# Folding the bias of v through one channel, and moving two small steps of the first batch

## The chip, the cores and the metric

The kernel runs on one core of a Trainium2 chip. A core has a matrix engine (TensorE, PE in the profile), a vector engine (VectorE, DVE), a scalar engine (ScalarE, ACT), a general engine (GpSimd, POOL) and a queue engine (SyncE, SP) that here only issues DMAs. Each engine runs its own instructions strictly in order and waits on semaphores for the others. The metric is the device time of one execution in microseconds (us), the median of several runs.

## The reference

The input x has 8 batches of 1024 rows and 256 channels. All in float32:

```
xn  = layernorm(x)                       # over the 256 channels, no scale or shift
qkv = xn @ qkv_w + qkv_b                 # 16 heads of 16 channels each
q, k = q/|q|, k/|k|                      # per row and head
kv  = einsum('bhnd,bhne->bhde', k, v)    # linear attention, no softmax
att = einsum('bhnd,bhde->bhne', q, kv) @ proj_w + proj_b
ffn = relu(xn @ W1 + b1) @ W2 + b2       # 256 -> 1024 -> 256
out = x + att + ffn
```

Since there is no softmax, v is never formed. With kn the normalised k, the kernel computes G = xn^T kn (256 x 256), then kv = Wv^T G + b_v (sum of kn). The bias term is had by changing both factors. If xn gets 1 added in some channels and the rows of Wv get a row vector a added, the product gains what b_v needs. It rests on the channels of xn summing to zero in every row, so that adding the same a to every row of Wv changes nothing by itself.

## The kernel before, in words

Rows are tiled by 128: a batch is 8 tiles, two halves of four. The large products (the hidden layer, the output, q and k, G) are made by a Strassen-like scheme with seven products in place of eight, called here "by sums": POOL builds sums and differences of blocks ahead of the matmuls, DVE adds the products together as they leave PSUM. Names in the trace: `pq*` are banks of the q/k projection, `ph*` of the hidden layer, `po*` of the output, `gp*` of G.

The program is one list written out by hand; the order in which the Python code issues instructions is the order on every engine. There is no planner.

Batch 0 is special. A prologue warms PE, normalises x of batch 0 on DVE and projects q and k in plain matmuls (`project`, L326). DVE adds the bias (L333), ACT squares (L342), DVE reduces the squares to sums per head (L343), and DVE also takes the statistics of the first half of batch 1 (L255, L258) meanwhile. Then comes `hidden(0)`, which walks a list of steps: `first(i)`, `fifth(i)` and `last(i)` for the four units i of the hidden layer (matmuls L658, DVE adds L670, ACT copies L684 and ReLUs L665). Behind each step the dictionary `first_steps` names small work to be issued: the norms of k (`norms_of_first`: L368 maximum on DVE, L371 square root on ACT, L374 reciprocal on DVE), the scaling of k and q by them on POOL (`scale`, L489), the normalisation of batch 1 (`norm_scale`: L267 and L270 on DVE; `norm_apply`: L279 on ACT), the addition of ones to x (`shift`, L518 on ACT), G of batch 0 in plain matmuls (`mix_g`, L525), the fold of v's bias (`fold_bias_of_v`: L505 on PE, L508 and L512 on DVE), the transposes of batch 1 (`turn_x`: L293 on DVE, L295 DMAs from SP), kv (`mix_kv`: L619 on PE, L625 on DVE) and M = kv proj_w (`mix_m`: L636, L640). The sums for the hidden layer's output are POOL's (`sums_of_a`, L192 to L196), and so are those of W2 (L188), of wq and wk (L381, L188) and of x of batch 1 (L229 to L241).

`mix_g` of batch 0 is a join: its first matmul needs k scaled by POOL and x of batch 0 with the ones that `shift` adds on ACT. Its matmuls stand on PE behind the fifth product of unit 1.

Later batches use `later_steps` and `shift(b + 2)` at their end; they differ from batch 0 in order only.

Of the kernel before, what the change touches and what calls it, by code (L numbers as in the profile page):

```python
# [9 lines left out]
F32 = mybir.dt.float32  # L10
AF = mybir.ActivationFunctionType
ALU = mybir.AluOpType
# [4 lines left out]
def kernel(  # L17
# [34 lines left out]
    nc = tc.nc  # L52
    P = 128
    B, N, C = x.shape
    H, D = 16, 16
    assert H * D == C
    INTER = w1.shape[1]
    NT = N // P
    HT = NT // 2
# [30 lines left out]
    def bank(shape, name):  # L90

        return psum.tile(shape, F32, tag="bank", name=name)
# [15 lines left out]
    def load_squares(b, halves=(0, 1)):  # L108
        xqs[b] = one.tile([P, 2, R, HT, CJ], F32, tag="xq", name=f"xq_{b}")
        for n in halves:  # L110
            for j in range(R):
                nc.sync.dma_start(out=xqs[b][ts(j, S), n], in_=squares_v(x, b, n, j))
# [25 lines left out]
    w2_sb = const.tile([P, FC, C], F32, tag="w2", name="w2_sb")  # L138
    ob = const.tile([P, 3, 2], F32, tag="ob", name="ob")

    def load_halves(dst, w):

        src = w.rearrange("(k p) (j m c) -> m j p k c", p=P, m=2, c=S)
        for m in range(2):
            for j in range(R):
                nc.sync.dma_start(out=dst[:, :, (m * R + j) * S : (m * R + j + 1) * S], in_=src[m, j])

    def load_rest():

        load_halves(w2_sb, w2)  # L150
        load_halves(projw_sb, proj_w)
        for i, v in enumerate((proj_b, b2)):
            for j in range(R):
                nc.sync.dma_start(
                    out=ob[ts(j, S), i, :],
                    in_=v.rearrange("(j m c) -> j c m", m=2, c=S)[j],
                )
# [107 lines left out]
    def norm_scale(b, tiles, on_act):  # L265
        i, mv, rstd = stats[b, tiles[0]]
        nc.vector.reciprocal(rstd, rstd)  # L267
        if on_act:
            nmr = small.tile([P, NT], F32, tag="nmr", name=f"nmr_{b}_{i}")[:, : len(tiles)]
            nc.vector.scalar_tensor_tensor(nmr, mv[:, :, 0], -1.0, rstd, ALU.mult, ALU.mult)  # L270
            for t in tiles:
                stats[b, t] += (nmr,)

    def norm_apply(b, tiles):
        for t in tiles:
            xt, xn = xs[b][:, t, :], xns[b][:, t, :]
            i, mv, rstd, *nmr = stats.pop((b, t))
            if nmr:
                nc.scalar.activation(  # L279
                    xn, xt, AF.Identity, bias=nmr[0][:, i : i + 1], scale=rstd[:, i : i + 1]  # L280
                )
            else:
                nc.vector.tensor_scalar(
                    xn, xt, mv[:, i, 0:1], rstd[:, i : i + 1], ALU.subtract, ALU.mult
                )
# [23 lines left out]
    def project(b, within={}, behind={}, held_to=0):  # L309

        xnT = xnTs[b]
        if b not in qks:
            qks[b] = one.tile([P, NT, 2 * C], F32, tag="qk", name=f"qk_{b}")
        qk = qks[b]
        late, held, adds = [], [], []
        for h in range(2):
            ss = small.tile([P, HT, 2 * H], F32, tag="ssk" if h else "ssq", name=f"ss_{b}_{h}", bufs=1)
            for s in range(2):  # L320
                norms_of[b, h, s] = ss[:, :, ts(s, H)]
            for i in range(HT):
                t = h * HT + i
                pq = bank([P, 512], f"pq_{b}_{t}")
                for kc in range(KC):
                    nc.tensor.matmul(  # L326
                        pq, xnT[:, kc, t // 2, :, t % 2], wqkv_sb[:, kc, 0 : 2 * C],
                        start=(kc == 0), stop=(kc == KC - 1), skip_group_check=True,
                    )
                    if kc == 0:  # L330
                        within.get(t, lambda: None)()
                adds.append(
                    lambda t=t, pq=pq: nc.vector.tensor_tensor(  # L333
                        qk[:, t, :], pq, qkvb_sb[:, 0 : 2 * C], ALU.add
                    )
                )
                while adds and t > 0:
                    adds.pop(0)()

                def square(t=t, ss=ss, i=i):  # L340
                    sq = work.tile([P, 2 * C], F32, tag="yt", name=f"sq_{b}_{t}")
                    nc.scalar.activation(sq, qk[:, t, :], AF.Square)  # L342
                    return lambda: nc.vector.tensor_reduce(  # L343
                        ss[:, i, :], sq.rearrange("p (g d) -> p g d", d=D), AX.X, ALU.add
                    )

                held.append(square)
                while held and t >= held_to:
                    late.append(held.pop(0)())
                    while len(late) > 1:  # L350
                        late.pop(0)()
                behind.get(t, lambda: None)()
        while late:
            late.pop(0)()

    norms_of = {}

    def invert(ss):

# [3 lines left out]

    def norms_of_first(s):

        parts = [norms_of[0, h, s] for h in range(2)]
        for p in parts:
            nc.vector.tensor_scalar_max(p, p, L2_EPS * L2_EPS)  # L368
        yield
        for p in parts:  # L370
            nc.scalar.activation(p, p, AF.Sqrt)  # L371
        yield
        for p in parts:
            nc.vector.reciprocal(p, p)  # L374
        yield

# [109 lines left out]
    def scale(eng, b, h, s):  # L486

        part = qks[b][:, ts(h, HT), ts(s, C)].rearrange("p t (g d) -> p t g d", d=D)
        eng.tensor_tensor(  # L489
            part, part,  # L490
            norms_of[b, h, s].unsqueeze(3).to_broadcast([P, HT, H, D]), ALU.mult,
        )
# [8 lines left out]
    def fold_bias_of_v():  # L501

        wv = wqkv_sb[:, :, of_v]
        of_rows = bank([P, C], "of_rows")
        nc.tensor.matmul(of_rows, mean, wv[:, 0, :], start=True, stop=True)  # L505
        yield
        a = one.tile([P, C], F32, tag="ksum", name="a")
        nc.vector.scalar_tensor_tensor(  # L508
            a, qkvb_sb[:, of_v], 1.0 / P, of_rows, ALU.mult, ALU.subtract
        )  # L510
        yield
        nc.vector.tensor_tensor(wv, wv, a.unsqueeze(1).to_broadcast([P, KC, C]), ALU.add)  # L512
        yield

    def shift(b):

        part = xns[b][:, :, 0:P]
        nc.scalar.activation(part, part, AF.Identity, bias=ones)  # L518

    def mix_g(b):  # L520
        qk, xn = qks[b], xns[b]
        gp = ps_mix.tile([P, KC, C], F32, tag="mix", name=f"gp_{b}")
        for f in range(KC):
            for t in range(NT):
                nc.tensor.matmul(  # L525
                    gp[:, f, :], xn[:, t, ts(f, P)], qk[:, t, C : 2 * C],
                    start=(t == 0), stop=(t == NT - 1),
                )
        gT = one.tile([P, KC, C], F32, tag="gT", name=f"gT_{b}")
        nc.scalar.copy(gT, gp)  # L530
        mixes[b] = gT
# [206 lines left out]
    def first_steps(b):  # L738

        lo, hi, fold = range(HT), range(HT, NT), fold_bias_of_v()  # L740
        of_k, of_q = norms_of_first(1), norms_of_first(0)
        return {
            0: [lambda: load_squares(b), lambda: norm_apply(b + 1, lo)],
            1: [lambda: next(of_k)] * 3 + [lambda h=h: scale(nc.gpsimd, b, h, 1) for h in range(2)],
            2: [lambda: shift(b)],
            4: [
                lambda: norm_stats(b + 1, hi), lambda: norm_scale(b + 1, hi, True),
                lambda: norm_apply(b + 1, hi), lambda: next(of_q), lambda: next(of_q),
                lambda: next(of_q), lambda: mix_g(b), lambda: next(fold),
            ] + [lambda: turn_x(b + 1)] * R,  # L750
            5: [lambda: next(fold), lambda: next(fold), sums_of_wqk, sum_of_biases]
            + [lambda h=h: scale(nc.gpsimd, b, h, 0) for h in range(2)],
            6: [lambda: shift(b + 1)],
            7: [lambda: mix_kv(b)],
            8: [lambda: g_sums(b + 1, 0)],
            10: [lambda: mix_m(b), lambda: turn_q(b)],
            11: [lambda: turn_q(b), lambda: load(b + 2)],
        }
# [212 lines left out]
    def tiles_4_to_7():  # L971
# [8 lines left out]
    of_next = norm_stats_steps(1, range(HT))  # L980
    project(
        0, {0: tile_1, 1: tiles_2_3, 3: tiles_4_to_7},
        {t: lambda n=n: [next(of_next) for _ in range(n)] for t, n in ((3, 1), (4, 1), (5, 1), (6, 2))}
        | {7: lambda: norm_scale(1, range(HT), True)},
        3,
    )
    load_rest()
    s3_of_x(0)
    sums_of_w2()
# [71 lines left out]
```

## Time and profile before

| | before |
|---|---|
| median of 3 runs (lowest to highest) | 613.55 us (613.02 to 614.63) |
| profiled execution, its time | 613.64 us |
| its span, first to last instruction | 611.8 us |
| busy: PE | 605.9 us (99%) |
| busy: DVE | 419.4 us (69%) |
| busy: ACT | 208.2 us (34%) |
| busy: POOL | 422.0 us (69%) |
| granted PE clock, mean | 0.999 |

The span is what the profiler sees between the first and the last instruction; the time is some 1.8 us longer. A row of a timeline gives the start in us, how long the merged instructions took, engine, line, operation, what is written and read by the program's names, and the count; idle time of the engine ahead of it, and what ended that, stand in square brackets. A busy PE is one that has a matmul in flight: in PE's rows the start of the next pass says more than the end of this one.

### The profile page before, as it was taken

To read this page: it belongs to the slowest core of one execution; us is meant where nothing else is said; L and a number is where in the kernel's file an instruction comes from. 1 tells how busy PE (TensorE), PEld (TensorE's weight loads), DVE (VectorE), ACT (ScalarE), POOL (GpSimd) and SP (SyncE) were. 2 spreads that over 40 slices of the span, in tenths; PEclk is the share of its full clock that TensorE was granted. 3 is DMA by queue.
4 is the path that set the end of the run, shared out by engine and by line. 5 is a ranking of instruction groups with operands and counts; after the bars stand their busy time and mean duration, and the time that the engine had idled before them with its cause. 6 is when DMAs were issued, how large, how long until landed. Compare 5 with 4: busy or idle time off the path is not lost.

```text
span 611.8 us, 6697 instructions
## 1 busy us (share of the span) xinstructions
PE 605.9 (99%) x2037; PEld 349.6 (57%) x2037; DVE 419.4 (69%) x751; ACT 208.2 (34%) x362; POOL 422.0 (69%) x346
## 2 busy tenths in 40 slices
PE   9999999999999999999999999999999999999996
PEld 6466664465644756448464484644755556645454
DVE  7987767877487764787557784687846777258824
ACT  4645214441334413343143520526205352023500
POOL 2899992699636995479934999259991599914700
PEclk9999999999999999999999999999999999999999
DMA  8543403750048300581005810158002640005202
GB/s 286 84 101 74 104 1 69 167 108 0 1 99 188 58 1 5 126 175 40 0 19 120 181 27 0 34 127 167 19 0 48 140 90 0 1 9 129 69 1 69
DMA packets 145315, 44.88 MB, mean 73 GB/s; under 512 B 141312, under 2 KB 142208, under 8 KB 145280
## 3 DMA queue, kind: packets, MB, share of 16 engines
q1 hardware_dynamic: 143648, 43.29, 32.1%
q10 hardware_dynamic: 1632, 1.18, 0.7%
q8 instruction: 16, 0.26, 0.2%
q14 instruction: 19, 0.16, 0.1%
HBM read 20.32 MB, written 8.39 MB: 47 GB/s over the span
## 4 chain that ended last, share of the span: by engine, by line
PE 96%; DVE 2%; POOL 0%; ACT 0%; issue 0%; DVEq 0%
PE poa L784 11%; PE poe L784 11%; PE pod L784 11%; PE pha L658 9%; PE phd L658 9%; PE phe L658 9%; PE poc L784 6%; PE phc L658 4%; PE pqd L415 4%; PE pqe L415 4%; PE pqa L415 4%; PE gpd L588 2%; PE gpe L588 2%; PE gpa L588 2%; PE pqc L415 2%; PE pq L326 1%
## 5 line engine op out<-in xcount | busy, mean ns | idle before, releaser
L822 POOL TENSOR_TENSOR xq<-xq,yt_o 128x512 f32<-128x512 f32 x29 | 36.8, 1267 | 124.0 <-DVE yt_o L816 124.0
L665 ACT ACTIVATE hT<-hT,b_sb 128x512 f32<-128x512 f32 x96 | 69.0, 721 | 61.4 <-DVE hT L670 56.4
L192 POOL TENSOR_TENSOR hS<-hT 128x512 f32<-128x512 f32 x31 | 46.5, 1500 | 32.5 <-ACT hT L665 32.5
L658 PE MATMUL pha<-xnT,w_sb 128*128 128x512 f32 x128 | 65.4, 592 | 0.0
L393 ACT ACTIVATE sq<-qk 128x512 f32<-128x512 f32 x56 | 34.2, 627 | 83.8 <-DVE qk L421 69.2
L784 PE MATMUL poa<-hT,w_sb 128*128 128x512 f32 x128 | 57.6, 592 | 0.0
L670 DVE TENSOR_TENSOR hT<-phe,u 128x512 f32<-128x512 f32 x64 | 43.7, 685 | 7.0 <-PE phe L658 5.2
L194 POOL TENSOR_TENSOR hS<-hT,hS 128x512 f32<-128x512 f32 x31 | 39.6, 1276 | 2.4
L193 POOL TENSOR_TENSOR hS<-hS,hT 128x512 f32<-128x512 f32 x31 | 39.5, 1273 | 2.4
L196 POOL TENSOR_TENSOR hT<-hT 128x512 f32<-128x512 f32 x31 | 40.0, 1289 | 0.0
L816 DVE STREAM_TRANSPOSE yt_o<-y_o 128x512 f32<-128x512 f32 x30 | 32.7, 1091 | 7.2 <-ACT y_o L877 5.0
L784 PEld LDWEIGHTS poa<-hT,w_sb 128*128 128x128 f32 x128 | 23.8, 190 | 24.2 <-issue 23.9
L658 PEld LDWEIGHTS pha<-xnT,w_sb 128*128 128x128 f32 x128 | 23.7, 190 | 22.9 <-issue 22.0
L670 DVE TENSOR_TENSOR u<-phc,u 128x512 f32<-128x512 f32 x32 | 21.7, 679 | 20.2 <-ACT u L684 11.1
L665 ACT ACTIVATE hT<-pha,b_sb 128x512 f32<-128x512 f32 x32 | 21.9, 683 | 35.5 <-PE pha L658 35.5
L658 PE MATMUL phd<-xnT,w1t 128*128 128x512 f32 x64 | 32.7, 592 | 0.0
L658 PE MATMUL phd<-xnT,w_sb 128*128 128x512 f32 x64 | 32.7, 592 | 0.0
L658 PE MATMUL phe<-xS,w1t 128*128 128x512 f32 x64 | 32.7, 592 | 0.0
L658 PE MATMUL phc<-xS,w1t 128*128 128x512 f32 x64 | 32.7, 592 | 0.0
L658 PE MATMUL phe<-xS,w_sb 128*128 128x512 f32 x64 | 32.7, 592 | 0.0
L684 ACT COPY u<-pha 128x512 f32<-128x512 f32 x32 | 18.4, 575 | 35.4 <-PE pha L658 35.4
L826 DVE SCALAR_TENSOR_TENSOR y_o<-poe,ob,u_o 128x512 f32<-128x512 f32 x15 | 11.3, 750 | 27.4 <-PE poe L784 26.5
(201 smaller groups left out, 1340.4 us busy)
## 6 DMA issues: line engine op xcount, KB each, us to landing
qT<-turn_q SPq DMA_DIRECT2D x128, 64.0 KB, 2.1
x<-in_L_attn_x_dram SPq DMA_DIRECT2D x15, 512.0 KB, 6.3
xq<-in_L_attn_x_dram SPq DMA_DIRECT2D x60, 128.0 KB, 3.6
out_dram<-xq SPq DMA_DIRECT2D x58, 128.0 KB, 2.7
xnT<-turn_x SPq DMA_DIRECT2D x112, 64.0 KB, 2.1
w_sb<-in_L_ffn_W_dram SPq DMA_DIRECT2D x2, 512.0 KB, 7.2
w_sb<-in_L_ffn_W_dram SPq DMA_DIRECT2D x8, 128.0 KB, 3.3
x<-in_L_attn_x_dram SPq DMA_DIRECT2D x3, 256.0 KB, 6.0
```

Of the source, the lines that this page charges most:

```text
L192: eng.tensor_tensor(s1, a21, a22, ALU.add)
L193: eng.tensor_tensor(s2, s1, a11, ALU.subtract)
L194: eng.tensor_tensor(s4, a12, s2, ALU.subtract)
L196: eng.tensor_tensor(a21, a11, a21, ALU.subtract)
L393: nc.scalar.activation(sq, part_of_qk(b, n, g, m), AF.Square)
L415: nc.tensor.matmul(dst[:, w, :], a[:, g, :, w], rhs, start=start and w == 0, stop=stop, skip_group_check=True,)
L588: nc.tensor.matmul(dst, l[:, t, :], r[:, t, :], start=start and t == 0, stop=stop and t == HT - 1, skip_group_check=True,)
L658: nc.tensor.matmul(dst, lhsT, rhs, start=start, stop=stop, skip_group_check=True)
L665: nc.scalar.activation(block(i, n, m), src, AF.Relu, bias=b1_sb[:, fc : fc + 1])
L670: nc.vector.tensor_tensor(dst, p, q, ALU.add)
L784: nc.tensor.matmul(dst, l, r, start=start and n == 0, stop=stop and n == len(lhs) - 1, skip_group_check=True,)
L822: eng.tensor_tensor(xh, xh, yt.rearrange("p u w r c -> p (u w) r c"), ALU.add)
```

## The change

Four things are changed. (1) `shift` adds ones to one channel of xn instead of to 128, in all batches. To match, the row that is added to Wv becomes a = b_v - (row 0 of Wv). That row is loaded from memory, broadcast to all partitions, by one more DMA in `load_rest`, so that the matmul that averaged rows of Wv is left out. The subtraction and the addition stand at other steps, and `mix_kv(0)` stands one step later. (2) The sums of squares of q and k of batch 0 lie in one tile for both halves, so the maximum and the square root are one instruction each. (3) The norms of k of batch 0 are issued at the end of the projection and at step 0, and no longer at step 1. (4) The reciprocal, the scaled mean and the normalisation of the first half of batch 1 are issued at step 2, behind `first(1)` and ahead of `shift(0)`; before, they stood in the projection and at step 0.

On each engine's queue this reads, in batch 0: PE loses the `of_rows` matmul, and `kvp` comes three products later. DVE has maximum, two adds of unit 0, the two reciprocals of k, the join `hT`, two adds of unit 1, then reciprocal and `nmr` of batch 1. ACT has the square root of k, the ReLU and the copy of unit 1, then four normalisations of batch 1 and the shift, then the ReLUs of unit 0. SP has one DMA more, ahead of the `ob` loads. POOL's order is the same.

```diff
+    a_sb = one.tile([P, C], F32, tag="ksum", name="a")
@@ load_rest
         load_halves(projw_sb, proj_w)
+        nc.sync.dma_start(out=a_sb, in_=qkv_w[0, of_v].partition_broadcast(P))
@@ project
-            ss = small.tile([P, HT, 2 * H], F32, tag="ssk" if h else "ssq", name=f"ss_{b}_{h}", bufs=1)
+            ss = ss_first[:, ts(h, HT), :]
@@
+    ss_first = one.tile([P, NT, 2 * H], F32, tag="M", name="ss_first")
@@ norms_of_first
-        parts = [norms_of[0, h, s] for h in range(2)]
-        for p in parts:
-            nc.vector.tensor_scalar_max(p, p, L2_EPS * L2_EPS)
+        ss = ss_first[:, :, ts(s, H)]
+        nc.vector.tensor_scalar_max(ss, ss, L2_EPS * L2_EPS)
         yield
-        for p in parts:
-            nc.scalar.activation(p, p, AF.Sqrt)
+        nc.scalar.activation(ss, ss, AF.Sqrt)
         yield
-        for p in parts:
+        for p in (norms_of[0, h, s] for h in range(2)):
             nc.vector.reciprocal(p, p)
@@ fold_bias_of_v
         wv = wqkv_sb[:, :, of_v]
-        of_rows = bank([P, C], "of_rows")
-        nc.tensor.matmul(of_rows, mean, wv[:, 0, :], start=True, stop=True)
+        nc.vector.tensor_tensor(a_sb, qkvb_sb[:, of_v], a_sb, ALU.subtract)
         yield
-        a = one.tile([P, C], F32, tag="ksum", name="a")
-        nc.vector.scalar_tensor_tensor(
-            a, qkvb_sb[:, of_v], 1.0 / P, of_rows, ALU.mult, ALU.subtract
-        )
+        nc.vector.tensor_tensor(wv, wv, a_sb.unsqueeze(1).to_broadcast([P, KC, C]), ALU.add)
         yield
-        nc.vector.tensor_tensor(wv, wv, a.unsqueeze(1).to_broadcast([P, KC, C]), ALU.add)
-        yield
@@ shift
-        part = xns[b][:, :, 0:P]
+        part = xns[b][:, :, 0:1]
         nc.scalar.activation(part, part, AF.Identity, bias=ones)
@@ first_steps
-        of_k, of_q = norms_of_first(1), norms_of_first(0)
+        of_q = norms_of_first(0)
         return {
-            0: [lambda: load_squares(b), lambda: norm_apply(b + 1, lo)],
-            1: [lambda: next(of_k)] * 3 + [lambda h=h: scale(nc.gpsimd, b, h, 1) for h in range(2)],
-            2: [lambda: shift(b)],
+            0: [lambda: load_squares(b), lambda: next(of_k), lambda: next(of_k)],
+            1: [lambda h=h: scale(nc.gpsimd, b, h, 1) for h in range(2)],
+            2: [
+                lambda: norm_scale(b + 1, lo, True), lambda: norm_apply(b + 1, lo),
+                lambda: shift(b),
+            ],
             4: [
                 lambda: norm_stats(b + 1, hi), lambda: norm_scale(b + 1, hi, True),
                 lambda: norm_apply(b + 1, hi), lambda: next(of_q), lambda: next(of_q),
-                lambda: next(of_q), lambda: mix_g(b), lambda: next(fold),
+                lambda: next(fold), lambda: next(of_q), lambda: mix_g(b),
             ] + [lambda: turn_x(b + 1)] * R,
-            5: [lambda: next(fold), lambda: next(fold), sums_of_wqk, sum_of_biases]
-            + [lambda h=h: scale(nc.gpsimd, b, h, 0) for h in range(2)],
+            5: [sums_of_wqk, sum_of_biases] + [lambda h=h: scale(nc.gpsimd, b, h, 0) for h in range(2)],
             6: [lambda: shift(b + 1)],
-            7: [lambda: mix_kv(b)],
-            8: [lambda: g_sums(b + 1, 0)],
+            7: [lambda: next(fold)],
+            8: [lambda: g_sums(b + 1, 0), lambda: mix_kv(b)],
@@ around project(0, ...)
-        {t: lambda n=n: [next(of_next) for _ in range(n)] for t, n in ((3, 1), (4, 1), (5, 1), (6, 2))}
-        | {7: lambda: norm_scale(1, range(HT), True)},
+        {t: lambda n=n: [next(of_next) for _ in range(n)] for t, n in ((3, 1), (4, 1), (5, 1), (6, 2))},
         3,
     )
+    of_k = norms_of_first(1)
+    next(of_k)
     load_rest()
```

## The prediction

> **What bounds the kernel now.** I read the page first: TensorE (PE) is busy 605.9 of the 611.8 us span at a granted clock of 0.999, and the chain that ended last is PE to 96%. The wait list of PE then has two rows only, 1.1 us at the very start and 0.3 us in the last piece. So a change can win little, namely instructions that it takes off PE and the few tenths in which PE stands still, and it can lose whatever wait it brings to PE. Everything that the diff moves lies in batch 0, between 24 and 60 us, so I read that stretch engine by engine. First PE in order of time (columns: start us, us, what, in brackets the idle time before and its releaser):
>
> ```profile
> 29.67 1.02 PE L658 MATMUL phe<-xS,w_sb 128*128 128x512 f32 x2
> 30.53 1.02 PE L658 MATMUL phe<-xS,w1t 128*128 128x512 f32 x2
> 31.64 7.34 PE L525 MATMUL gp<-qk,x 128*128 128x256 f32 x32
> 38.82 0.59 PE L505 MATMUL of_rows<-wqkv_sb,mean 128*128 128x256 f32 x2
> 39.25 1.02 PE L658 MATMUL pha<-xnT,w_sb 128*128 128x512 f32 x2
> ```
>
> Starts follow each other at 0.43 us per 128x512 pass and 0.216 per 128x256 pass. The `phe` pair from 30.53 therefore leaves PE free at 31.39, and `gp` starts at 31.64: 0.25 us of waiting for POOL's scaling of k. `gp` is the join: it needs the scaled k and the x of batch 0 that `shift` (L518) has written. What `shift` stands behind on ScalarE (ACT) decides this change:
>
> ```profile
> 24.88 2.08 ACT L279 ACTIVATE x<-x,nmr,rstd 128x256 f32<-128x256 f32 x4
> 27.66 0.72 ACT L665 ACTIVATE hT<-hT,b_sb 128x512 f32<-128x512 f32 x1 [0.71 <-DVE hT L670]
> 28.73 0.40 ACT L371 ACTIVATE ss<-ss 128x64 f32<-128x64 f32 x2 [0.35 <-DVE ss L368]
> 29.04 0.57 ACT L684 COPY u<-pha 128x512 f32<-128x512 f32 x1
> 29.51 1.15 ACT L518 ACTIVATE x<-x,ones 128x1024 f32<-128x1024 f32 x1
> 30.56 0.68 ACT L665 ACTIVATE hT<-pha,b_sb 128x512 f32<-128x512 f32 x1
> ```
>
> The shift ends at 30.66, 0.7 us before PE could use it. The four `x` of batch 1 are normalised long before, at 24.88. VectorE (DVE) in the same stretch:
>
> ```profile
> 24.40 0.44 DVE L270 SCALAR_TENSOR_TENSOR nmr<-mv,rstd 128x4 f32<-128x4 f32 x1
> 24.76 0.67 DVE L343 TENSOR_REDUCE ss<-sq 128x32 f32<-128x512 f32 x1
> 25.36 0.67 DVE L670 TENSOR_TENSOR u<-phc,u 128x512 f32<-128x512 f32 x1
> 26.14 0.69 DVE L670 TENSOR_TENSOR u<-phd,u 128x512 f32<-128x512 f32 x1
> 26.93 0.69 DVE L670 TENSOR_TENSOR hT<-phe,u 128x512 f32<-128x512 f32 x1
> 27.54 1.25 DVE L368 TENSOR_SCALAR ss<-ss 128x64 f32<-128x64 f32 x2
> 29.02 0.96 DVE L374 RECIPROCAL ss<-ss 128x64 f32<-128x64 f32 x2 [0.22 <-ACT ss L371]
> ```
>
> And GpSimd (POOL), whose instructions also tell how long some of DVE's last:
>
> ```profile
> 24.90 1.28 POOL L188 TENSOR_TENSOR w2t<-w_sb,w2t 128x512 f32<-128x512 f32 x1
> ...
> 27.37 1.28 POOL L188 TENSOR_TENSOR w2t<-w_sb,w2t 128x512 f32<-128x512 f32 x1
> 29.65 3.83 POOL L489 TENSOR_TENSOR qk<-qk,ss 128x1024 f32<-128x1024 f32 x2 [1.00 <-DVE ss L374]
> 33.44 1.27 POOL L192 TENSOR_TENSOR hS<-hT 128x512 f32<-128x512 f32 x1
> ...
> 56.87 1.28 POOL L241 TENSOR_TENSOR xnT<-xnT 128x512 f32<-128x512 f32 x1
> ```
>
> The `max` of L368 that starts at 27.54 lasts 1.155 us, its twins 0.180. It ends as POOL's instruction from 27.37 ends (28.65). The rows of L360 show the same for the 128x128 form: 1.0 us where POOL works, 0.226 where it rests.
>
> ```profile
> L360 DVE TENSOR_SCALAR ssk<-ssk x7: 1001/1016/1027, 70.6 to 515.7; 128x128 f32<-128x128 f32 x7
> L360 DVE TENSOR_SCALAR ssq<-ssq x7: 226/226/227, 99.5 to 539.5; 128x128 f32<-128x128 f32 x7
> L270 DVE SCALAR_TENSOR_TENSOR nmr<-mv,rstd x8: 200/218/1646, 24.4 to 452.2; 128x8 f32<-128x8 f32 x6, 128x4 f32<-128x4 f32 x2
> ```
>
> `nmr` is held in the same way: 0.79 us from 35.28 to POOL's end at 36.06, 1.65 us from 81.13 to POOL's end at 82.75. I call this a hold.
>
> **The change, part by part.** I rebuild batch 0 with the durations above; one engine's end becomes another's start after 0.05 us (`hT` ends on DVE at 27.62, ACT starts at 27.66).
>
> *Taken off PE.* `of_rows` goes: 39.25 - 38.82 = -0.43 us.
>
> *The norms of k ahead of the join.* The reciprocal and `nmr` of batch 1 leave 24.20 to 24.76, so the last reduce waits only for its square (23.78 + 0.63): 24.45 to 25.13. The merged 128x128 `max` is issued at 25.18, inside POOL's sum from 24.90 to 26.18: held, it ends near 26.26 instead of 25.40. `u` then starts at 26.18 (before: 25.36), the second `u` at 26.96, and the two reciprocals, now ahead of the `hT` join, take 0.47 + 0.41 from 27.57. The join starts at 28.45 and ends at 29.14, 1.5 us later than now. What the earlier norms bring: POOL can scale k as soon as its own w2 sums end, 28.65 to 32.48 rather than 29.65 to 33.48. That removes the 0.25 us wait and two pauses of 0.10 inside `gp` (passes at 0.320 instead of 0.216, POOL's second half): -0.46 us, if nothing else is late.
>
> *xn of batch 1 behind the second unit.* Something else is late. Queued on ACT behind the late join: its ReLU at 29.18, the copy of the second unit's `u` at 29.80 to 30.37 (before: 29.04). DVE adds to that `u` at 30.41 and 31.14 (step 0.73 as now), then the moved reciprocal at 31.75 (0.20), then `nmr` at 31.95. POOL is in its second scaling (30.54 to 32.48), so `nmr` is held to 32.50; free it would end at 32.15. ACT then does the four normalisations, moved here, at 0.49 us each from 32.55, and only behind them `shift`. It starts at 34.51. Its new form 128x8 is not in the trace; the nearest rows are ACT's 128x4 at 0.30 and 128x64 at 0.24, against 1.14 now. With 0.30 it ends at 34.81 and `gp` starts at 34.86, where PE was free at 31.39: a wait of 3.47 us. PE's own chain thus gives 3.47 - 0.46 - 0.43 = +2.6 us. Without the hold on `nmr` it is +2.2; with no hold at all (`nmr` 31.13 to 31.30, `gp` at 33.65) it is 2.26 - 0.89 = +1.4. The largest hold on the `max`, 1.28 us if it is issued just as POOL starts, would add 0.45 to the 0.83 taken: `nmr` is then issued at 32.40 and ends at 32.57, `gp` starts at 34.93, +2.7.
>
> *Behind that wait on ACT* stand the ReLUs of the first unit, which POOL's `hS` sums need: the second ReLU ends at 36.07, `hS` starts at 36.12 instead of 33.44, +2.7. POOL works without a pause from there to L241 at 56.87, and PE takes `pqd` at 58.21 when L241 ends (58.15), with 0.03 us to spare. So POOL's delay reaches PE there. The new subtraction for `a` reads two SBUF tiles beside those sums. The fold's addition L512, of that kind, took 1.37 us now and the scaling beside it 4.27 instead of 3.83, so POOL may lose 0 to 0.44 more; I take 0.3: POOL +3.0.
>
> *The rest costs nothing that I can see.* One more DMA on SP (0.48 us of issue at 25.3) goes ahead of the `ob` and `xq` loads, whose last issue ends at 36 and whose successor, the turn of batch 1, comes at 39.9 or later. The nearest broadcast took 5.6 us to land, so `a` is there at 31, seven us before DVE wants it; were it 8 us late, DVE's turn of x would follow. The fold's addition moves behind the three `hT` adds that PE's second unit releases. Shifted by 2.8 us, these end near 48.5; with its 1.37 the fold ends near 49.8. `kvp` moves with it, behind three matmul pairs of the fourth unit, to about 50.3 (before 46.15 + 3 x 0.86 = 48.7 without `kvp`'s own 0.89, so 47.8, and 2.6 later). Its cover is half a us, and what goes beyond it PE would wait. The smaller `shift` frees 0.84 us of ACT in each later batch, where PE does not wait for it.
>
> **Sum.** PE pays the later of two chains, +2.6 or +3.0, of which 0.3 is the uncertain hold: I take +2.8. On the profiled execution, 611.8 us of span and 613.64 in time, that is 616.44; the median before is 0.09 lower, so the forecast is 616.4.
>
> Two rules of the Trainium skill bear on this. "SBUF — State Buffer", Who interferes with whom, says that a VectorE instruction with two SBUF inputs fully blocks on a GpSimd instruction that reads SBUF; the row L270 has a median of 0.218 us beside busy POOL, which looks like no hold, but those six were issued within 0.2 us of POOL's end and decide nothing. By the rule PE's chain is +2.6, by that median +2.2. "TensorE: Matmul & The Clock Gate", What's actually happening and Why this matters for your kernels, warns of PE gaps over about 3 us, a window of 3.4 us after which the clock falls to half; no row of this trace has such a gap in the middle. By that rule an estimate would add half of a 3.4 us window, 1.7 us, for 618.1; I leave it to a rival.
>
> **Rivals.**
> 1. *No hold* (0.12). The two DVE instructions slip between POOL's: +1.4, 615.0. For it: 0.18 and 0.226 us are what they cost alone, and POOL's phase hangs on a DMA's landing at 23.5. Against: POOL is busy in 24 to 28 and in the scaling.
> 2. *The clock falls in the gap* (0.08). At the start PE ran at half pace for 5.7 us (passes of 0.213 us for 128 columns from 1.05 to 6.78, 0.110 after). That again after `gp` loses 2.9 us: 619.3. Against: there PE had done nothing before; here it has been full for 25 us.
> 3. *The shift is not last* (0.05), the other side. Then both gains stay: 613.55 - 0.89 = 612.7. It needs `nmr` done by 29.0, so that four normalisations (1.97) and the shift (0.30) fit before 31.39. For it: the statistics are ready at 23.45. Against: on DVE `nmr` is now behind the second unit's `u`, whose source PE delivers after 27.
>
> **How the numbers follow.** The forecast has 0.75, with its own range 615.5 to 617.6 (+2.0 to +4.0, which also takes in the spread of 613.02 to 614.63 shown for one kernel). The range for 8 in 10 reaches down to the no-hold case and stops short of the other two: 614.8 to 618.0. A measurement of this kernel tells about 0.3%, 1.84 us. Slower by more: 0.75 and 0.08, and a little of rival 1, 0.85; within: rival 1 and rival 3, 0.13; faster: 0.02, since even rival 3 gains only 0.15%.
>
> **What would show it.** In the profile after: one PE wait of 3 to 3.7 us ahead of `gp`, released by ACT's write of `x`; `nmr` near 32 ending with POOL's second scaling; four normalisations right before the shift; POOL's first `hS` near 36; a PE wait of some 0.4 at `pqd` released by POOL `xnT`; no `of_rows`. I am wrong if `gp` starts before 33, if PE's passes after it run at 0.43 for 256 columns, or if a PE wait appears in the later batches.

## The result and the profile after

The changed kernel took 617.38 us (median of 6 runs, 616.46 to 619.07), the kernel before in the same session 613.41 us (6 runs, 612.92 to 614.63): a ratio of 1.0064, with a 95% interval of 1.0052 to 1.0076. That is 4.0 us slower. The forecast was 616.4 with a range of 614.8 to 618.0.

The profiled execution has a span of 615.5 us and a time of 617.51. The waits of PE (engine, tile and line, what it waited for, total us, times, longest) have one new row of more than 0.2 us:

```profile
PE gp L521 <- ACT x L514: 2.9, 1, 2.9
```

PE in order of time around it:

```profile
30.45 1.02 PE L654 MATMUL phe<-xS,w1t 128*128 128x512 f32 x2
34.40 8.83 PE L521 MATMUL gp<-qk,x 128*128 128x256 f32 x32 [2.93 <-ACT x L514]
43.07 1.02 PE L654 MATMUL pha<-xnT,w_sb 128*128 128x512 f32 x2
...
51.65 1.05 PE L615 MATMUL kvp<-gT,wqkv_sb 128*128 128x128 f32 x8
...
62.01 1.03 PE L417 MATMUL pqd<-wqkv_sb,xnT 128*128 128x256 f32 x4
```

PE is free at 31.31 and starts `gp` at 34.40, 3.09 us later. `gp` then takes 8.83 us where it took 7.34, although it starts with every operand ready. The next view says why. It gives the busy time of each engine in a stretch (start:end and length, then PE, PE's weight loads, DVE, ACT and POOL with their counts), the granted PE clock and the DMA share; the three rows are the gap, the 3.4 us after its first passes, and the 3.4 us after those:

```profile
31.40:34.40 3.00, 0.07 (x2) 0.03 (x1) 2.97 (x8) 2.42 (x6) 0.53 (x1) 1.00 0.82 176
34.90:38.30 3.40, 3.40 (x10) 2.64 (x9) 1.82 (x9) 2.07 (x5) 2.63 (x3) 0.50 0.69 100
38.30:41.70 3.40, 3.40 (x17) 3.01 (x16) 1.53 (x4) 2.15 (x5) 3.40 (x4) 0.99 0.01 1
```

The clock fell to 0.50 after the gap, for one stretch of 3.4 us: 10 passes where the next stretch has 17. Eight passes follow after 0.40 to 0.43 us instead of 0.216, a loss of 1.7 us. ACT, DVE and POOL show the chain that made the gap, in this order:

```profile
28.61 0.72 ACT L661 ACTIVATE hT<-hT,b_sb 128x512 f32<-128x512 f32 x1 [2.50 <-DVE hT L666]
29.24 0.57 ACT L680 COPY u<-pha 128x512 f32<-128x512 f32 x1
31.98 2.07 ACT L282 ACTIVATE x<-x,nmr,rstd 128x256 f32<-128x256 f32 x4 [2.17 <-DVE nmr L273]
33.96 0.29 ACT L514 ACTIVATE x<-x,ones 128x8 f32<-128x8 f32 x1
...
34.73 1.93 ACT L661 ACTIVATE hT<-hT,b_sb 128x512 f32<-128x512 f32 x3
```

```profile
25.08 0.69 DVE L371 TENSOR_SCALAR ss_first<-ss_first 128x128 f32<-128x128 f32 x1
...
27.95 0.63 DVE L666 TENSOR_TENSOR hT<-phe,u 128x512 f32<-128x512 f32 x1
29.84 0.69 DVE L666 TENSOR_TENSOR u<-phc,u 128x512 f32<-128x512 f32 x1 [1.26 <-ACT u L680]
...
31.45 0.50 DVE L273 SCALAR_TENSOR_TENSOR nmr<-mv,rstd 128x4 f32<-128x4 f32 x1
```

```profile
24.42 1.27 POOL L191 TENSOR_TENSOR w2t<-w_sb,w2t 128x512 f32<-128x512 f32 x1
...
28.10 3.83 POOL L491 TENSOR_TENSOR qk<-qk,ss_first 128x1024 f32<-128x1024 f32 x2
35.52 1.27 POOL L195 TENSOR_TENSOR hS<-hT 128x512 f32<-128x512 f32 x1 [3.59 <-ACT hT L661]
...
49.08 1.27 POOL L195 TENSOR_TENSOR hS<-hT 128x512 f32<-128x512 f32 x1 [0.62 <-ACT hT L661]
...
59.73 1.28 POOL L244 TENSOR_TENSOR xnT<-xnT 128x512 f32<-128x512 f32 x1
```

The maximum issued at 25.08 lasts 0.69 us, to the end of POOL's sum (24.42 + 1.27 = 25.69); the late join, the late copy, `nmr` held to the end of POOL's scaling (28.10 + 3.83 = 31.93), the four normalisations and only then the shift follow as the prediction has them. POOL rests 3.59 us for the ReLUs behind the shift, and its last sum ahead of `pqd` ends at 61.01 instead of 58.15, 2.9 us later. PE is 3.8 us late there (62.01 against 58.21), so POOL is no longer waited for in this execution. Part of POOL's delay comes from PE itself: 0.62 us of it is the pause at 49.08, in which POOL waits for a ReLU whose products PE's slow passes had made late.

The six runs of the changed kernel are not alike. Two have a granted clock of 0.999 and took 616.46 and 616.65; four have 0.992 to 0.997 and took 617.25 to 619.07. One stretch of 3.4 us at half the clock takes 0.003 off the mean of such a span, so the fallen clock seems to come in some executions of one program and not in others. Only one of the six has a profile that shows it; the run at 0.992 would need more than one such stretch.

### The profile page after: what moved, and what is told of

It is laid out like the page before. It is cut to its first block, busy times and chain, and to the rows that moved or that the text cites. A ratio compares the mean times of both kernels' runs of the same rounds, so it can differ in the third digit from the quotient of the medians.

```text
span 615.5 us, 6691 instructions
## 1 busy us (share of the span) xinstructions
PE 606.3 (99%) x2035; PEld 349.6 (57%) x2035; DVE 417.4 (68%) x749; ACT 201.2 (33%) x360; POOL 422.0 (69%) x346
## 4 chain that ended last, share of the span: by engine, by line
PE 96%; DVE 2%; DMA 0%; ACT 0%; issue 0%
PE poa L782 11%; PE poe L782 11%; PE pod L782 10%; PE pha L654 9%; PE phd L654 9%; PE phe L654 9%; PE poc L782 6%; PE phc L654 4%; PE pqe L417 4%; PE pqa L417 4%; PE pqd L417 4%; PE gpe L584 2%; PE gpd L584 2%; PE gpa L584 2%; PE pqc L417 2%; PE gp L521 1%
```

## The experiments

Two chains were suspected, and one more cause beside them. Chain one: the shift stands on ACT behind four normalisations, and PE's `gp` waits for it. Chain two: the ReLUs stand behind the same normalisations, POOL's sums for the hidden layer wait for them, and PE meets POOL's delay some 25 us later, in the projection of batch 1. The third is PE's clock, which falls after the gap. The first four kernels in the list that follows were compared with 15 runs of the kernel before (median 613.41 us, 612.81 to 613.90); the half-filled gap, the single parts and the lighter POOL with 27 (613.35); the last two with 15 (613.39).

### The shift ahead of the normalisations

```diff
             2: [
-                lambda: norm_scale(b + 1, lo, True), lambda: norm_apply(b + 1, lo),
                 lambda: shift(b),
+                lambda: norm_scale(b + 1, lo, True), lambda: norm_apply(b + 1, lo),
             ],
```

> The changed kernel with the shift of batch 0 ahead of the moved reciprocal, nmr and four normalisations; nothing else differs. Theory A (two chains: the shift's place on ACT, and the ReLUs behind the normalisations that hold POOL's hS sums back): the 2.9 us wait at gp goes, gp starts near 31.4, but POOL's hS still starts near 35.2 against 33.44 before, so PE meets the delay later, in one or several waits of together some 2.5 us between 44 and 60 us, released by POOL's sums or by DVE: 615.0 to 616.4, that is +1.8 to +3.0 on before. Rival B (the shift alone costs): no PE wait after gp, both gains stay, 612.5 (-0.9).

It took 615.82 us (5 runs, 615.48 to 617.03), a ratio of 1.0044 (1.0031 to 1.0058). The wait at `gp` is gone, and the loss is not. PE in order of time, and below it POOL:

```profile
30.47 1.02 PE L654 MATMUL phe<-xS,w1t 128*128 128x512 f32 x2
31.32 4.91 PE L521 MATMUL gp<-qk,x 128*128 128x256 f32 x22
...
57.41 1.14 PE L417 MATMUL pqe<-wt,xS 128*128 128x256 f32 x4
58.76 1.14 PE L417 MATMUL pqc<-wt,xS 128*128 128x256 f32 x4 [0.22 <-POOL xS L233]
59.99 1.14 PE L417 MATMUL pqd<-wqkv_sb,xnT 128*128 128x256 f32 x4
```

```profile
34.97 1.27 POOL L195 TENSOR_TENSOR hS<-hT 128x512 f32<-128x512 f32 x1 [3.39 <-ACT hT L661]
47.89 1.72 POOL L195 TENSOR_TENSOR hS<-hT 128x512 f32<-128x512 f32 x1
58.66 1.27 POOL L244 TENSOR_TENSOR xnT<-xnT 128x512 f32<-128x512 f32 x1
```

`gp` follows `phe` with no pause (the first view's window ends inside `gp`, after 22 of its 32 passes). PE then stands 1.8 us at `kvp` (the pass before it is followed after 2.20 us instead of 0.43), which waits for DVE's addition for the fold:

```profile
46.33 2.15 DVE L508 TENSOR_TENSOR wqkv_sb<-wqkv_sb,a 128x512 f32<-128x512 f32 x1
```

The addition is held by POOL: it ends 0.55 us after POOL's scaling of q does (44.11 + 3.82 = 47.93). In the next experiment's profile the scaling ends at 46.10 and the addition at 46.64, and PE hardly waits. PE then loses 1.1 us in all around `pqe`, `pqc` and `pqd`, which start when POOL's sums end. Both waits come from POOL's delay: against the next experiment its scaling ends 1.83 us later, its last sum 1.82 (59.93 against 58.11), and PE is 1.83 late at `pqa` (56.42 against 54.59). So theory A holds and the rival, 612.5 us, falls. The shift's place is where the wait shows; the ReLUs behind the normalisations, for which POOL rests 3.39 us, are a second way to the same loss.

### xn of batch 1 back in its place

```diff
-            0: [lambda: load_squares(b), lambda: next(of_k), lambda: next(of_k)],
+            0: [lambda: load_squares(b), lambda: next(of_k), lambda: norm_apply(b + 1, lo), lambda: next(of_k)],
             1: [lambda h=h: scale(nc.gpsimd, b, h, 1) for h in range(2)],
-            2: [
-                lambda: norm_scale(b + 1, lo, True), lambda: norm_apply(b + 1, lo),
-                lambda: shift(b),
-            ],
+            2: [lambda: shift(b)],
...
+        | {7: lambda: norm_scale(1, range(HT), True)},
```

> The changed kernel with the moved reciprocal and nmr back in the projection and the four normalisations back at step 0 (behind the square root of k); the fold through one channel and the early norms of k stay. Theory A: the move carries the whole loss; the 0.43 us of the matmul left out and the 0.46 us of waits come off PE's chain, but POOL's sums, which reach L241 in before with 0.03 us to spare, give back what PE gains: 612.7 to 613.7 (-0.7 to +0.3), with PE waits of 0.3 to 0.8 us at pqc or pqd. Rival (the fold or the early norms cost by themselves): above 614.5, with a PE wait at kvp for the fold or at gp.

It took 613.75 us (11 runs, 613.07 to 614.16), a ratio of 1.0006 (0.9997 to 1.0015): the whole loss is gone (the median is 0.05 us above the range that I gave). What PE gained at `gp` does not show either. PE is 0.9 us ahead of the kernel before at `pqe` (55.58 against 56.46) and gives it back to POOL:

```profile
30.33 1.02 PE L654 MATMUL phe<-xS,w1t 128*128 128x512 f32 x2
31.19 5.13 PE L521 MATMUL gp<-qk,x 128*128 128x256 f32 x23
...
55.58 1.14 PE L417 MATMUL pqe<-wt,xS 128*128 128x256 f32 x4
56.94 1.14 PE L417 MATMUL pqc<-wt,xS 128*128 128x256 f32 x4 [0.22 <-POOL xS L233]
58.17 1.14 PE L417 MATMUL pqd<-wqkv_sb,xnT 128*128 128x256 f32 x4
```

`pqd` starts at 58.17, where it started at 58.21 before the change.

### That move alone, on the kernel before

The shift is still 128 channels wide here.

```diff
-            0: [lambda: load_squares(b), lambda: norm_apply(b + 1, lo)],
+            0: [lambda: load_squares(b)],
...
-            2: [lambda: shift(b)],
+            2: [
+                lambda: norm_scale(b + 1, lo, True), lambda: norm_apply(b + 1, lo),
+                lambda: shift(b),
+            ],
...
-        | {7: lambda: norm_scale(1, range(HT), True)},
```

> The kernel before with that move alone (shift still 128 channels wide, 1.14 us; of_rows and the norms of k as before). Theory A: a PE wait of 3 to 4 us at gp released by the shift, +2.5 to +3.5, and where the clock falls up to 1.7 more: 616 to 618.5. Rival (the loss needs the earlier join of the changed kernel): a wait under 1.5 us and below 614.5.

It took 617.47 us (5 runs, 615.83 to 617.69), a ratio of 1.0062 (1.0049 to 1.0075), as much as the whole change. The profiled execution happens to be the one at full clock, 615.83 us, with `gp` as follows (the window ends after its seventh pass):

```profile
30.53 1.02 PE L658 MATMUL phe<-xS,w1t 128*128 128x512 f32 x2
34.45 1.75 PE L525 MATMUL gp<-qk,x 128*128 128x256 f32 x7 [2.90 <-ACT x L518]
```

The wait is 3.06 us, as in the changed kernel, but the passes behind it keep their 0.216 us (7 in 1.75 us), and the mean clock is 1.000. The other four runs have clocks of 0.996 and 0.997 and took 617.32 to 617.69: 1.5 to 1.9 us more, about what one stretch at half the clock costs PE; they have no profile. It shows in full here because POOL is not the later chain: its last sum ends at 60.29 (59.01 + 1.28), half a us before PE takes `pqd` at 60.80. The expected 616 to 618.5 holds at the median.

### The gap filled

```diff
         gp = ps_mix.tile([P, KC, C], F32, tag="mix", name=f"gp_{b}")
+        for _ in range(6):
+            nc.tensor.matmul(gp[:, 0, :], ident, w1_sb[:, 0, 0:C], start=True, stop=True)
```

The fillers add work; what they write is overwritten by `gp`'s first pass.

> The changed kernel with six matmuls of 128x256 (12 passes, 2.6 us) that write zeros of no use into gp's bank ahead of gp, in PE's gap. Theory C (PE's clock falls because it idles near 3 us): no passes of gp at 0.43 us, granted clock 0.999 in every run, a rest of the wait at gp of 0.3 to 0.5, then a PE wait of 0.5 to 0.9 at pqd for POOL's L241; 616.3 (+2.9), 0.9 below the changed kernel's median and less scattered. Rival (gp's slow passes come from reads beside POOL or DMA, not from the idle time): slow passes stay, 617.3.

It took 615.88 us (5 runs, 615.56 to 616.84), a ratio of 1.0043 (1.0031 to 1.0056), with clocks of 0.998 to 1.000. PE in time, then the same stretch as above (engines' busy time, clock, DMA):

```profile
31.34 2.75 PE L520 MATMUL gp<-w_sb,ident 128*128 128x256 f32 x12
33.96 2.40 PE L523 MATMUL gp<-qk,x 128*128 128x256 f32 x10
...
60.13 1.14 PE L417 MATMUL pqd<-wqkv_sb,xnT 128*128 128x256 f32 x4
```

```profile
34.90:38.30 3.40, 3.40 (x17) 3.01 (x16) 1.71 (x4) 2.06 (x6) 3.07 (x3) 1.00 0.89 142
```

With matmuls in the gap the clock stays at 1.00, 17 passes go where 10 went, and the kernel is 1.5 us faster than the changed one though PE does more. Not all of that is the clock's: POOL's sums stood 0.44 us earlier in this execution, the maximum took 0.23 us instead of 0.69, and the shift ended at 33.81 instead of 34.25. POOL and DMA are no less busy than in that row of the changed kernel, so the rival (reads beside them) falls. What remains, +2.5 us, is less than my 616.3, since `gp` could follow the fillers at once; PE then waits 0.25 us for POOL at `pqd`.

### The gap half filled

```diff
-        for _ in range(6):
+        for _ in range(3):
```

> The changed kernel with three filling matmuls (1.3 us) in place of six: PE idles 1.4 to 1.8 us ahead of gp, not 2.9. If the clock falls only after some 3 us without a matmul, no pass of gp takes 0.43 us and the time is that of the filled gap, 615.5 to 616.5, in all runs. If any idle time near 1.5 us is enough, slow passes show in some runs and the median is 616.5 or more.

It took 616.48 us (5 runs, 616.39 to 617.80), a ratio of 1.0055 (1.0042 to 1.0068). The profiled execution had a gap of 2.0 us and a clock of 1.00 in the stretch behind it. PE, and below it POOL:

```profile
34.49 7.14 PE L523 MATMUL gp<-qk,x 128*128 128x256 f32 x32 [1.86 <-ACT x L514]
...
59.55 1.03 PE L417 MATMUL pqc<-wt,xS 128*128 128x256 f32 x4
60.63 1.14 PE L417 MATMUL pqd<-wqkv_sb,xnT 128*128 128x256 f32 x4
```

```profile
59.30 1.28 POOL L244 TENSOR_TENSOR xnT<-xnT 128x512 f32<-128x512 f32 x1
```

This is the closest view of the changed kernel without the fallen clock: the shift ends at 34.34 and `gp` starts at 34.49, within 0.1 us of the changed kernel's, and the execution took 616.39 us against 617.51. PE waits 0.22 us for POOL's last sum at `pqd`. Four runs lie within 616.39 and 616.65 with clocks of 0.999 or 1.000; the fifth took 617.80 at 0.997. So a gap of this length mostly leaves the clock alone. Whether it did in the fifth run isn't shown: that run has no profile, and a mean of 0.997 also stands beside 613.05 us, the fastest run of the kernel with POOL lighter and the fold of before. How long a gap is safe stays open.

### The fold alone, the early norms alone

Two runs put one part each on the kernel before: the fold through one channel with its load, its steps, the narrow shift and the later `kvp`; and the one tile of sums of squares with the early maximum, square root and reciprocal. Of the change's diff they take these lines (and the functions that the lines call):

```diff
+        nc.sync.dma_start(out=a_sb, in_=qkv_w[0, of_v].partition_broadcast(P))
-        nc.tensor.matmul(of_rows, mean, wv[:, 0, :], start=True, stop=True)
+        nc.vector.tensor_tensor(a_sb, qkvb_sb[:, of_v], a_sb, ALU.subtract)
-        part = xns[b][:, :, 0:P]
+        part = xns[b][:, :, 0:1]
-            7: [lambda: mix_kv(b)],
-            8: [lambda: g_sums(b + 1, 0)],
+            7: [lambda: next(fold)],
+            8: [lambda: g_sums(b + 1, 0), lambda: mix_kv(b)],
```

```diff
+            ss = ss_first[:, ts(h, HT), :]
...
-            0: [lambda: load_squares(b), lambda: norm_apply(b + 1, lo)],
-            1: [lambda: next(of_k)] * 3 + [lambda h=h: scale(nc.gpsimd, b, h, 1) for h in range(2)],
+            0: [lambda: load_squares(b), lambda: next(of_k), lambda: norm_apply(b + 1, lo), lambda: next(of_k)],
+            1: [lambda h=h: scale(nc.gpsimd, b, h, 1) for h in range(2)],
...
+    of_k = norms_of_first(1)
+    next(of_k)
     load_rest()
```

> The kernel before with the fold through one channel alone (its load, its subtraction and addition at their new steps, the shift of one channel, kvp one step later). Two-chain theory: of_rows is gone from PE (-0.43), but POOL's sums reach L241 no earlier, and the subtraction and the addition hold POOL up to 0.5 us, so PE waits 0.4 to 0.9 us at pqc or pqd: 613.0 to 614.0. Rival (the matmul left out is a gain): no such wait and 612.98 or less.

> The kernel before with the early norms of k alone (one tile of sums of squares, maximum at the end of the projection; of_rows, the wide shift and the place of batch 1's xn as before, the four normalisations behind the square root). Two-chain theory: gp's waits of 0.46 us go, POOL's hS starts when the ReLU is ready, some 0.2 us earlier than now at most, so PE keeps 0.1 to 0.4 and waits for L241 for the rest: 612.9 to 613.5. Rival (the waits at gp are a gain in full): 612.9 or less and no wait at pqc or pqd.

The fold alone took 613.82 us (11 runs, 613.24 to 614.45; 1.0006, 0.9997 to 1.0015), the norms alone 613.34 (11 runs, 612.80 to 613.93; 0.9999, 0.9990 to 1.0007), against 613.35 for 27 runs of before. Both are no change that can be told. The fold's PE stops for POOL as expected:

```profile
55.98 1.03 PE L418 MATMUL pqe<-wt,xS 128*128 128x256 f32 x4
57.07 1.14 PE L418 MATMUL pqc<-wt,xS 128*128 128x256 f32 x4
58.30 1.14 PE L418 MATMUL pqd<-wqkv_sb,xnT 128*128 128x256 f32 x4
```

These three should start 0.86 us apart; they are 1.09 and 1.23 apart, and the 0.43 us of the matmul left out are given back. With the norms alone PE waits at `gp` too, 0.17 us for the shift that is still 128 channels wide.

### POOL made lighter

On the kernel with the xn of batch 1 back in its place, two of POOL's sums go into pauses that POOL has anyway:

```diff
     s3_of_x(0)
+    dbias_of_qk()
     sums_of_w2()
...
-            1: [lambda h=h: scale(nc.gpsimd, b, h, 1) for h in range(2)],
+            1: [lambda h=h: scale(nc.gpsimd, b, h, 1) for h in range(2)] + [lambda: sums_of_wqk(0)],
...
-            5: [sums_of_wqk, sum_of_biases] + [lambda h=h: scale(nc.gpsimd, b, h, 0) for h in range(2)],
+            5: [lambda: sums_of_wqk(1), sum_of_biases] + [lambda h=h: scale(nc.gpsimd, b, h, 0) for h in range(2)],
```

`dbias_of_qk` is the difference of the biases (0.72 us), `sums_of_wqk(0)` the first of the four sums of wq and wk (0.73 us), `sums_of_wqk(1)` the other three.

> As the run with the xn of batch 1 back in its place, and two of POOL's sums for wq and wk (0.72 and 0.73 us) taken from between the two sets of hS sums into POOL's pauses: one ahead of the W2 sums, one behind the scaling of k. Two-chain theory: POOL's L241 ends 1.0 to 1.4 us earlier, the waits at pqe, pqc and pqd (0.9 us in sum) go, and what PE had gained shows: 612.4 to 613.0, 0.7 to 1.0 below that run and 0.4 to 0.9 below before. Rival (POOL is not what gives it back): no change against that run, 613.4 to 614.1.

It took 612.53 us (11 runs, 612.13 to 612.86), a ratio of 0.9985 (0.9976 to 0.9994): 1.2 us below the kernel without this edit, and below both kernels of this study. POOL's last sum ends 1.4 us earlier than there (55.47 + 1.28 = 56.75 against 58.11), and PE runs through:

```profile
55.47 1.03 PE L420 MATMUL pqe<-wt,xS 128*128 128x256 f32 x4
56.34 1.03 PE L420 MATMUL pqc<-wt,xS 128*128 128x256 f32 x4
57.20 1.03 PE L420 MATMUL pqd<-wqkv_sb,xnT 128*128 128x256 f32 x4
```

So it was POOL that took back PE's gain.

### POOL lighter, with the fold of before

```diff
-        nc.vector.tensor_tensor(a_sb, qkvb_sb[:, of_v], a_sb, ALU.subtract)
+        nc.tensor.matmul(of_rows, mean, wv[:, 0, :], start=True, stop=True)
...
-        part = xns[b][:, :, 0:1]
+        part = xns[b][:, :, 0:P]
...
+            5: [lambda: next(fold), lambda: next(fold), lambda: sums_of_wqk(1), sum_of_biases]
...
-            7: [lambda: next(fold)],
-            8: [lambda: g_sums(b + 1, 0), lambda: mix_kv(b)],
+            7: [lambda: mix_kv(b)],
+            8: [lambda: g_sums(b + 1, 0)],
```

> As the run with POOL's two sums moved, but with the fold of before (of_rows on PE, the wide shift, kvp a step earlier); the early norms stay. If the matmul left out is worth its 0.43 us as soon as POOL gives PE room, this is 0.3 to 0.5 us above that run: 612.8 to 613.1. If the fold is worth nothing even then (its holds on POOL eat it), the same as that run, 612.4 to 612.6.

It took 613.30 us (11 runs, 613.05 to 613.74; 0.9997, 0.9988 to 1.0006), 0.77 us above the run with the new fold and above both expectations. The matmul explains 0.43. PE's rows show two waits more. At `gp` it is 0.22 us (PE is free at 31.21, `gp` starts at 31.43), for the shift that is 128 channels wide again; at `kvp` it is 0.23 us (44.86, 45.09), for the fold's addition. ACT, DVE and POOL:

```profile
30.14 1.15 ACT L520 ACTIVATE x<-x,ones 128x1024 f32<-128x1024 f32 x1
```

```profile
43.27 1.68 DVE L514 TENSOR_TENSOR wqkv_sb<-wqkv_sb,a 128x512 f32<-128x512 f32 x1
```

```profile
46.38 1.27 POOL L192 TENSOR_TENSOR hS<-hT 128x512 f32<-128x512 f32 x1 [1.98 <-ACT hT L667]
```

The addition's old place, ahead of DVE's three `hT` adds, also gives POOL a pause, since with the new fold the same sum starts at 44.82. That pause costs no time here: POOL's last sum ends at 57.99 and PE takes `pqd` at 58.10. So the fold's part of the change is worth something, matmul, narrow shift and place, once POOL is not in the way.

### The W2 sums behind the scaling of k

The edit is on the changed kernel; it ran once.

```diff
     s3_of_x(0)
-    sums_of_w2()
...
-            1: [lambda h=h: scale(nc.gpsimd, b, h, 1) for h in range(2)],
+            1: [lambda h=h: scale(nc.gpsimd, b, h, 1) for h in range(2)] + [sums_of_w2],
```

> The changed kernel with POOL's four W2 sums behind the scaling of k, so that POOL rests while DVE takes the maximum and works while DVE takes nmr. Theory of the hold (a DVE instruction of these kinds waits for the end of POOL's running instruction): the maximum takes 0.23 us where it took 0.69, and nmr, issued inside a W2 sum, 0.6 to 1.4 us where it took 0.50, to the end of that sum; so the wait at gp stays near 3 us. Rival (0.69 us is the length of the merged 128x128 maximum): 0.69 again and nmr near 0.2 to 0.5.

```profile
25.14 0.23 DVE L371 TENSOR_SCALAR ss_first<-ss_first 128x128 f32<-128x128 f32 x1
...
31.04 0.16 DVE L273 SCALAR_TENSOR_TENSOR nmr<-mv,rstd 128x4 f32<-128x4 f32 x1
```

The maximum takes 0.23 us with POOL at rest: the hold is shown for it. For `nmr` I missed: it was issued at 31.04, just as POOL's scaling ended, and took 0.16 us, which is what it costs free. The wait at `gp` falls from 3.1 to 2.3 us, and yet the one time, 616.86, and the span, 614.8, are near the changed kernel's: PE loses 0.5 us at `kvp`, where the fold's addition is held to 49.62, and 1.1 around `pqe` to `pqd`, since POOL's `hS` sums now stand behind the W2 sums.

## Why the prediction was right

Sign, place and chain were right, and the size was 1.0 us too small, nearly all of it the clock that the forecast gave to a rival. That the median still lies in the range owes something to luck: the range was drawn to stop short of a falling clock, and one of the six runs (619.07) lies beyond it. By its own steps:

- *`of_rows` off PE*: -0.43 us, as read.
- *Early norms*: POOL's scaling moved from 29.65 to 28.10 and `gp`'s old waits of 0.46 us went. The scaling moved further than the predicted 28.65, since the W2 sums began 0.47 us earlier in that execution (23.07 against 23.54, when a DMA landed).
- *The wait for the shift*: 3.09 us against 3.47. The links stand where they were put, each a little earlier: the maximum ended at 25.77 (predicted 26.26), the join at 28.58 (29.14), `nmr` at 31.95 (32.50), the shift at 34.25 (34.81). The difference is POOL's earlier start; both holds end with POOL's instruction.
- *The narrow shift*: 0.29 us, predicted 0.30.
- *PE's own chain* without the clock is then 3.09 - 0.46 - 0.43 = +2.2, predicted +2.6, and 0.1 less by a prologue that ended earlier.
- *POOL's chain*: +2.86 at its last sum, predicted +3.0, and here the agreement is partly luck. The first `hS` came 2.08 us later than before, not 2.7, for POOL's earlier start again. The new holds took 0.60 from POOL (0.27 and 0.33 on two `hS` sums) instead of 0.3. The old hold's 0.44 came back, as the scaling beside the fold's old place took 3.83 instead of 4.27; the forecast had not taken that off. And 0.62 is the pause that PE's slow passes made. Where the clock held, in the half-filled kernel's profile, POOL's last sum is 2.43 us late (60.58 against 58.15) and PE 2.23 at `pqc` (59.55 against 57.32): POOL's chain is the later one, as forecast, by 0.2.
- *The sum without the clock*: the two runs at 0.999 are +3.1 and +3.2, the median of the half-filled kernel +3.1, that of the filled one +2.5, around the forecast's +2.8. Some 0.2 us of the changed kernel's loss lie outside the span (its times are 2.0 to 2.15 us longer than their spans, those of before 1.7 to 1.9), and no view shows why.
- *The clock*, rival 2, is the term that was mis-sized. The forecast gave it 0.08 and 2.9 us; judged by the mean clock and the time, it came in four of six runs of the changed kernel and in four of five with the move alone. It costs 1.7 us on PE, of which some 1.1 show: the four runs have a median of 617.6, the two others 616.46 and 616.65. PE that keeps its clock waits for POOL in part of that time, 0.22 us in the half-filled kernel; with the move alone, where POOL is not the later chain, the difference is 1.5 to 1.9. The estimate worked from the Trainium skill's "TensorE: Matmul & The Clock Gate" (What's actually happening) was 1.7 us, half of a window of 3.4 us, and this trace has the stretch (34.9 to 38.3 at 0.50) and the loss. I had set it aside because no row of before showed a gap, and had taken the kernel's start as the nearest row. That row misled: its slow passes last longer, and the profile's clock reads 1.00 there. The page's limit (Why this matters for your kernels), about 3 us without matmuls, agrees with the gap of 3.1 us behind which the clock fell in this trace. The same gap in the profile of the move alone was followed by a clock of 1.00, and no run here shows what decides.
- *The fold's half us of cover* held in the changed kernel (`kvp` starts at 51.65 in PE's stride) and did not where PE came earlier: 1.8 us of wait with the shift first.
- *Rivals 1 and 3* did not come. Rival 3's two gains exist, as the kernel with POOL made lighter shows, but moving the shift alone does not reach them: the ReLUs and POOL would have asked the price. Its 612.7 us left out chain two.

The wait of 0.4 us at `pqd`, which the forecast wanted to see, is not in the changed kernel's profile, as PE was too late for it; it is there, at 0.22 and 0.25 us, with the gap half filled and filled. And one of the forecast's signs of being wrong did come: passes of `gp` at 0.43 us.

## What to carry to other kernels

Before a small step is moved to a "free" engine's later place, list what stands behind it in that queue: here a shift and four ReLUs, two ways by which 2 us of normalising became 3 us of waiting. Where an engine is 99% busy, look for the second one that is only just in time (POOL's sum ended 0.06 us before PE took it): nothing taken off the first shows until the second is lighter. And an idle gap near 3 us on PE can cost half as much again behind it (here 1.7 us of passes, some 1.1 us of time), so it is worth trying to fill it with any matmul if it can't be closed.

## What the runs showed of the hardware

- PE's clock, 1.00 in the profile up to the gap, went to 0.50 for 3.4 us after a gap of 3.1 us, starting 0.5 us after work had resumed. The same gap in another execution of nearly the same program left it at 1.00. With matmuls in the gap the mean clock of five runs was 0.998 to 1.000.
- A VectorE maximum over 128x128 in SBUF takes 0.23 us with GpSimd at rest and 0.69 us when issued 0.6 us before the end of a GpSimd sum; `nmr`, with two SBUF operands, takes 0.16 us free and 0.50 held to the end of GpSimd's scaling. The Trainium skill's "SBUF — State Buffer" (Who interferes with whom) describes an exclusive lock for VectorE instructions with two SBUF inputs, and for the maximum's kind in some modes. `nmr`'s pair agrees; the maximum was held, and no run shows its mode.
- The hold goes both ways: POOL's `hS` sum of 1.27 us took 1.72 beside DVE's addition for the fold. That addition ended 0.55 us after the POOL instruction inside which it was issued, so it took 2.15 us when issued 1.60 us before the end of that instruction (shift first), 1.02 at 0.47 (changed kernel) and 0.83 at 0.28 (gap half filled).
